# Inverting the softmax sums of a fused attention kernel: a whole-tile reciprocal, or two block transposes around a reciprocal of one column in 32

## The chip, the cores and the metric

The kernel runs on one core of a Trainium2 chip. The metric is the device time of one execution in microseconds. The engines are named as in the profile: PE (TensorE, matrix products), DVE (VectorE), ACT (ScalarE), POOL (GpSimd) and SP (SyncE, which here issues DMAs). [...]

## What is computed

Eight images of 256 channels and 32x32 points pass through two layers. Layer 0 is an attention of 8 heads of 32 channels: all 1024 points ask, and 1426 keys and values answer, which come from pooled and convolved maps. Layer 1 is an attention with one head over the 1024 points of each image, followed by eight experts of three matrix products each. The change touches only the softmax of layer 0:

```python
attn = jax.nn.softmax(jnp.einsum('bhqd,bhkd->bhqk', q_g, k) * SCALE, axis=-1)
out_att = jnp.einsum('bhqk,bhkd->bhqd', attn, v)
```

The kernel forms the exponentials without subtracting a maximum, multiplies them with the values, and divides the product by the sum of the exponentials afterwards. A checksum of the sums and of their inverses is kept (`hi` and `lo`), from which the end of the program decides whether a slower, general path has to be taken.

## The kernel before

**Units and steps.** Attention of layer 0 works through 32 units: 8 images (`b`), 2 halves of the channels (`c`, four heads each), and 2 halves of the queries (`sl`, 512 each). A unit has 11 steps, one for each block of 128 keys, and each image has one more step for the keys left over. In a step, PE forms the scores of four heads (`scores`, tile `sc`, four PSUM banks and only one such tile), ACT takes the exponential of all 2048 columns into a tile `pt`, and PE multiplies the exponentials of the step before with the values (`values`, into `pv`). The next step's scores need `sc` free, so they wait for this step's exponential.

**The sums.** The tiles `pt` are added up pairwise by DMAs that add as they write (`add`), then by DVE (`sums`, line 1571). When all are added, `sums` lets PE multiply the total with a matrix of ones, `kit.ones[:, :DH]`, one head into each group of 32 PSUM rows. So each group of 32 rows holds 32 equal copies of one head's sums for the 512 queries. This tile, `total`, takes one of the small PSUM banks: there are two with the tag `sm` and one with the tag `sx`, and every other small product uses the same three.

Before the change, ACT copies `total` to the SBUF tile `rec` and adds up the checksum on the way (line 1587). `normalise` (line 1590) inverts all 512 columns of `rec` on DVE, multiplies the unit's result `att` with it, and lets ACT run over `rec` once more for the second checksum. Then `unit` (line 1875) counts the unit as done, and after an image's last unit starts `project(b)`, the output projection, on which layer 1 of this image waits.

**The planner.** Nothing of this order is found at run time. While the program is being built, a class `Flow` keeps a clock for every engine and the state of every tile; `cost` (line 723) estimates each operation, `note` (line 765) moves the clocks and fixes each engine's order. Work beside the steps lives in generators ("threads") with a rank: the units' sums have rank 0, projection 1, keys and values 2 to 4, layer 1's output 5 and 6, the convolution's taps on DVE 7. A thread says what it needs next by a `yield`: `pe(tile)`, `ve(tile)` or `act(tile)` name the engine and the tiles that must be ready. `runnable` (line 855) lets a thread continue if the engine's planned clock is not too far ahead of PE's: at most 4.0 us for DVE and 2.0 us for ACT (`AHEAD`, line 36). For PE it asks for credit: each step gives 4.0 us to the threads of rank below 5 and 2.0 us to the others (`PACE`, `PACE1`), and lets work through without credit when the planned end of the exponential leaves PE more than 1 us to spare. A small bank counts as taken for good from its allocation until the first instruction that reads it has been planned (`open`, lines 711 and 808).

Two lines of `cost` price the operations at hand: `reciprocal` costs 0.1 + 0.0064 us for each column, and any other operation of DVE without a line of its own, a transpose too, costs 0.15 + 0.00107 us for each column.

After the steps comes the experts' stage, which begins by running the first two expert layers while layer 1 of the last image is still being worked on.

All recorded instructions have line 670 in the profile, that of the helper that calls the engine. So groups are told apart by the names of their tiles: `rec<-sm` and `rec<-sx` are ACT's copies of the sums (and, with 256 columns on DVE, layer 1's own reciprocal), `rec<-rec` is the reciprocal on DVE and the second checksum on ACT, `att<-att,rec` the product.

Of the kernel before, what the change touches and what calls it, by code (L numbers as in the profile page):

```python
# [10 lines left out]
AF = mybir.ActivationFunctionType  # L11
# [5 lines left out]
P = 128  # L17
# [3 lines left out]
DH = 32  # L21
# [891 lines left out]
def attention(tc, kit, f, outer, ended, nb, consts, x, t1, t2, hn, bounds, vecs, q_t, kv_t, proj_t, gqk_t, wqk, wqkv, vecs1, w1_d, w1c, gate_d, wrc, vecs2, bnvec):  # L913
# [6 lines left out]
    with ExitStack() as ctx:  # L920
        l1, shared = outer
        wp = ctx.enter_context(tc.tile_pool(name="w0", bufs=1))
        work = ctx.enter_context(tc.tile_pool(name="work0", bufs=1))
        psum = ctx.enter_context(tc.tile_pool(name="psum0", bufs=1, space=PSUM))

        def T(pool, shape, tag, bufs=1):
            return f.tile(pool, shape, tag, bufs=bufs)

        def small():
            if f.also and f.free("sx") < min(map(f.end, f.slots.get("sm", [None]))):  # L930
                return T(psum, [P, 512], "sx")
            return T(shared, [P, 512], "sm", bufs=2)
# [46 lines left out]
        hi, lo = bounds  # L979
        for t in bounds:  # L980
            f.pool.memset(t, 0.0)
        column = [4 * (n // 4 * 2) + n % 4 for n in range(4 * nb)]
# [108 lines left out]
        def pe(*tiles, tag=None):  # L1091
            return "PE", tiles, tag

        def ve(*tiles):
            return "DVE", tiles, None

        def act(*tiles, tag=None):
            return "ACT", tiles, tag
# [7 lines left out]
        def until(cond):  # L1106
            return None, cond, None
# [463 lines left out]
        def sums(n, pairs):  # L1571

            for i in range(1, NKC // 2):
                yield until(lambda: len(pairs) > i)
                for j in range(0, 4, 2):
                    s = pairs[0][:, j : j + 2, :]
                    yield ve(s, pairs[i])
                    f.ve.tensor_tensor(s, s, pairs[i][:, j : j + 2, :], ALU.add)
            yield until(lambda: normalised[0] == n)
            yield pe(pairs[0], tag="sm")  # L1580
            total = small()
            for j in range(4):
                f.pe.matmul(
                    total[DH * j : DH * j + DH, :], lhsT=kit.ones[:, :DH], rhs=pairs[0][:, j, :], start=True, stop=True
                )
            rec = T(work, [P, 512], "rec")
            f.act.activation(rec, total, AF.Copy, accum_out=hi[:, column[n] : column[n] + 1])
            return rec

        def normalise(b, c, sl, rec, n):  # L1590
            att = atts[b, c][:, sl]
            yield ve(rec)
            f.ve.reciprocal(rec, rec)
            f.ve.tensor_tensor(att, att, rec, ALU.mult)
            yield act(rec)
            f.act.activation(rec, rec, AF.Copy, accum_out=lo[:, column[n] : column[n] + 1])

        def project(b):
            if b == nb - 1:
                last = T(work, [P, 2, HW], "pt", bufs=6)  # L1600
                f.sp.dma_start(last, x[b].rearrange("(k p) n -> p k n", p=P))
            for m in range(2):
                for half in range(2):
                    sl = slice(half * 512, half * 512 + 512)
                    xt = last[:, m, sl] if b == nb - 1 else T(work, [P, 512], "xr")
                    yield pe(atts[b, 0], atts[b, 1], xt, tag="sm")
                    ps = small()
                    for c in range(2):
                        f.pe.matmul(
                            ps, lhsT=mt[:, c, m * P : (m + 1) * P], rhs=atts[b, c][:, sl], start=c == 0, stop=c == 1  # L1610
                        )
                    if b == nb - 1:
                        yield ve(ps, xt)
                        f.ve.scalar_tensor_tensor(xt, ps, bias[:, m : m + 1], xt, ALU.add, ALU.add)
                    else:

                        yield act(ps)
                        f.act.activation(xt, ps, AF.Identity, bias=bias[:, m : m + 1])
                        yield pool(xt)
                        f.pool.dma_start(out=t1[b][:, m, sl], in_=xt, accum_op=ALU.add)  # L1620
            if b == nb - 1:
                f.sp.dma_start(t1[b], last)
            projected[0] += 1
# [249 lines left out]
        mt = T(wp, [P, 2, C], "mt")  # L1873
        bias = T(wp, [P, 2], "mtb")
        def unit(b, c, sl, n, pairs):
            rec = yield from sums(n, pairs)
            yield from normalise(b, c, sl, rec, n)
            normalised[0] += 1
            if c and sl.start:
                f.spawn(project(b), 1)  # L1880

        atts = {}
# [21 lines left out]
        for i in range(len(steps) + 1):  # L1904
            if i < len(steps):
                b, c, half, kc = steps[i]
                sl = slice(half * 512, half * 512 + 512)
# [18 lines left out]
            if i and steps[i - 1][3] < NKC - 1:  # L1926
                b1, c1, half1, kc1 = steps[i - 1]
                if kc1 == 0:
                    pv = T(psum, [P, 512], "pv")
                    pairs = []  # L1930
                    sl1 = slice(half1 * 512, half1 * 512 + 512)
                    f.spawn(unit(b1, c1, sl1, units, pairs), 0)
                    units += 1
                f.finish(lambda: kc1 // 4 in vts[b1])
                values(b1, c1, kc1, pts[i - 1], pv)
                if kc1 % 2:
                    add(kc1, pts.pop(i - 1), pts[i - 2])
                    pairs.append(pts.pop(i - 2))
                if kc1 == NKC - 2:
                    u = 2 * c1 + half1  # L1940
                    tail_values(b1, u, pv)
                    pairs.append(pts.pop(i - 1))
                    tail_add(u, pairs[-1])
                    f.finish(lambda: projected[0] >= b1)
                    f.act.activation(atts[b1, c1][:, sl1], pv, AF.Copy)
# [510 lines left out]
def tile_conv_attn_hybrid(  # L2456
# [45 lines left out]
    with ExitStack() as early:  # L2502
        l1 = early.enter_context(tc.tile_pool(name="l1", bufs=1, side="right"))
        shared = early.enter_context(tc.tile_pool(name="psum_l1", bufs=1, space=PSUM, side="right"))
        f = Flow(tc, kit)

        ended = [0]
        attention(
            tc, kit, f, (l1, shared), ended, nb,
            consts, x, t1, t2, hn, bounds, vecs0, q_t, kv_t, proj_t, gqk_t, wqk, wqkv, vecs1, w1_d, w1c, gate_d, wrc, vecs2, bnvec,  # L2510
        )
        last(f, (l1, shared), ended, early)
# [122 lines left out]
```

## Time and profile before

| What | us |
|---|---|
| median of 3 runs | 3240.89 (3236.12 to 3240.96) |
| profiled execution | 3236.82 |
| its span, first to last instruction | 3235.0 |
| PE busy | 3064.9 (95%) |
| DVE busy | 2458.7 (76%) |
| ACT busy | 1692.2 (52%) |
| POOL busy | 1198.6 (37%) |

Attention of layer 0 lies between about 162 and 1875 us of the span. In the profile's forty slices PE stands at 7 to 9 tenths there and at 8 to 9 after it, and the granted clock of PE is at full speed but for one slice near 120 us. A group's line gives the line of code, engine and operation, the tiles, their shapes and how many there were; then, after a bar, the busy time in us and the mean of one in ns; and after a second bar the engine's idle time just before them and what ended it. A line of waits gives who waited for whom, the total in us, how often, and the longest.

### The profile page before, as it was taken

To read this page: it belongs to the slowest core of one execution; us is meant where nothing else is said; L and a number is where in the kernel's file an instruction comes from. 1 tells how busy PE (TensorE), PEld (TensorE's weight loads), DVE (VectorE), ACT (ScalarE), POOL (GpSimd) and SP (SyncE) were. 2 spreads that over 40 slices of the span, in tenths; PEclk is the share of its full clock that TensorE was granted. 3 is DMA by queue.
4 is the path that set the end of the run, shared out by engine and by line. 5 is a ranking of instruction groups with operands and counts; after the bars stand their busy time and mean duration, and the time that the engine had idled before them with its cause. 6 is when DMAs were issued, how large, how long until landed. Compare 5 with 4: busy or idle time off the path is not lost.

```text
span 3235.0 us, 55827 instructions
## 1 busy us (share of the span) xinstructions
PE 3064.9 (95%) x22342; PEld 1793.5 (55%) x22342; DVE 2458.7 (76%) x4064; ACT 1692.2 (52%) x2302; POOL 1198.6 (37%) x1293
## 2 busy tenths in 40 slices
PE   8787899999999999989999999999999999999998
PEld 3422234334334334333433367777888888888887
DVE  5787787987898889988754546346888788777776
ACT  3476676576657666676665523334333333444443
POOL 2312314214232232241111210006756666777775
PEclk9799999999999999999999999999999999999999
DMA  1277656665665565764676653124444442000000
GB/s 51 72 157 169 133 115 146 142 138 122 132 152 121 128 144 120 172 144 88 152 161 128 154 205 134 55 90 163 150 143 150 150 163 72 20 30 23 20 14 21
DMA packets 117196, 375.49 MB, mean 116 GB/s; under 512 B 14512, under 2 KB 40440, under 8 KB 93696
## 3 DMA queue, kind: packets, MB, share of 16 engines
q0 software_dynamic: 28608, 179.85, 28.7%
q1 hardware_dynamic: 84960, 190.01, 17.3%
q8 instruction: 178, 2.92, 0.4%
q10 hardware_dynamic: 3360, 1.97, 0.2%
q14 instruction: 90, 0.74, 0.1%
HBM read 118.74 MB, written 87.60 MB: 64 GB/s over the span
## 4 chain that ended last, share of the span: by engine, by line
PE 71%; DVE 10%; ACT 7%; DMA 4%; issue 4%; POOL 2%; ACTq 0%; DVEq 0%; POOLq 0%; SPq 0%
PE bank L670 22%; PE sm L670 17%; PE y L670 10%; PE sc L670 8%; PE sx L670 8%; PE pv L670 6%; ACT pt L670 5%; DMA pt<-pt 3%; DVE acc L670 3%; DVE rec L670 1%; DVE pt L670 1%; DVE h L670 1%; DMA pt<-ptail 1%; DVE c L670 1%; DVE u L670 1%
## 5 line engine op out<-in xcount | busy, mean ns | idle before, releaser
L670 ACT ACTIVATE pt<-sc 128x2048 f32<-128x2048 f32 x352 | 660.7, 1877 | 269.3 <-PE sc L670 226.8
L670 DVE SCALAR_TENSOR_TENSOR acc<-p,vec,acc 128x961 f32<-128x961 f32 (+3 forms) x960 | 554.9, 586 | 32.0 <-ACT acc L670 6.4
L670 PE MATMUL sc<-q,kn 32*128 32x512 f32 (+1 forms) x3072 | 417.3, 644 | 102.0 <-ACT pt L670 97.9
L670 DVE TENSOR_TENSOR pt<-pt,pt 128x1024 f32<-128x1024 f32 x320 | 388.1, 1260 | 125.6 <-DMA pt<-pt 110.4
L670 PE MATMUL pv<-pt,vt 128*32 128x512 f32 x2816 | 380.1, 612 | 0.1
L670 ACT ACTIVATE p1c<-bank 128x256 f32<-128x256 f32 x226 | 86.6, 383 | 556.2 <-PE bank L670 550.2
L670 ACT ACTIVATE h<-h,bnvec 128x512 f32<-128x512 f32 x452 | 341.9, 805 | 62.7 <-DVE h L670 52.6
L670 POOL DMA_DIRECT2D pt<-pt x160 | 146.1, 913 | 561.2 <-ACT pt L670 438.5
L670 POOL TENSOR_TENSOR rstd<-rstd,mhalf 128x4 f32<-128x4 f32 (+2 forms) x88 | 107.5, 1222 | 624.1 <-DVE rstd L670 592.4
L670 DVE TENSOR_TENSOR h<-p1c,bank 128x512 f32<-128x512 f32 x226 | 154.1, 682 | 222.9 <-PE bank L670 216.0
L670 PEld LDWEIGHTS sc<-q,kn 32*128 32x128 f32 (+1 forms) x3072 | 113.6, 178 | 293.4 <-ACT pt L670 195.8
L670 POOL TENSOR_TENSOR tm<-h,tm 128x256 f32<-128x256 f32 x202 | 234.7, 1162 | 15.8
L670 DVE TENSOR_TENSOR h<-u,bank 128x256 f32<-128x256 f32 x452 | 230.2, 550 | 7.8
L670 PEld LDWEIGHTS pv<-pt,vt 128*32 128x32 f32 x2816 | 55.6, 108 | 271.8 <-issue 257.1
L670 PE MATMUL bank<-h,w2e 128*128 128x256 f32 (+1 forms) x620 | 203.6, 457 | 2.8 <-DVE h L670 1.9
L670 POOL TENSOR_TENSOR tm<-h 128x512 f32<-128x512 f32 x101 | 131.8, 1304 | 189.6 <-ACT h L670 189.6
L670 DVE TENSOR_TENSOR h<-h,gate 128x1024 f32<-128x1024 f32 x128 | 199.6, 1560 | 0.5 <-ACT h L670 0.5
L670 PE MATMUL y<-t,s3e 128*128 128x256 f32 x768 | 187.0, 379 | 1.9 <-POOL t L670 1.7
L670 PE MATMUL bank<-t,s1e 128*128 128x256 f32 x750 | 182.5, 379 | 0.2 <-DVE h L670 0.2
L670 POOL TENSOR_TENSOR t<-h 128x512 f32<-128x512 f32 x104 | 135.0, 1298 | 110.3 <-DVE h L670 93.3
L670 PE MATMUL sm<-y,t 128*32 128x256 f32 (+1 forms) x1976 | 175.6, 379 | 0.1
L670 DVE TENSOR_TENSOR u<-h,bank 128x512 f32<-128x512 f32 x226 | 155.5, 688 | 24.7 <-DVE h L670 0.9
(315 smaller groups left out, 5551.8 us busy)
## 6 DMA issues: line engine op xcount, KB each, us to landing
pt<-pt POOLq DMA_DIRECT2D x160, 1024.0 KB, 7.8
h<-h SPq DMA_DIRECT2D x142, 512.0 KB
xi<-in_x_dram SPq DMA_DIRECT2D x16, 512.0 KB
t<-t SPq DMA_DIRECT2D x8, 1024.0 KB
res<-t SPq DMA_DIRECT2D x32, 256.0 KB
t<-res SPq DMA_DIRECT2D x32, 256.0 KB
hn<-res SPq DMA_DIRECT2D x32, 256.0 KB
hn<-hn SPq DMA_DIRECT2D x16, 512.0 KB
```

The costliest lines, as they stand in the source:

```text
L670: ins = fn(*args, **kwargs)
```

## The change

`sums` hands back the PSUM tile `total` and no longer copies it. `normalise` lets DVE transpose `total` into `rec`: DVE's transpose works on blocks of 32x32, so block j of a row group now has in its rows the 32 queries of that block and in each of its 32 columns the same sum. ACT then copies `total` onto itself in PSUM, which only serves the first checksum. DVE inverts one column of each block, 16 columns in all, into a small tile `one`, and transposes `one`, read 32 times over, back into all of `rec`. The product with `att` and the second checksum are unchanged.

```diff
@@ sums @@
-            rec = T(work, [P, 512], "rec")
-            f.act.activation(rec, total, AF.Copy, accum_out=hi[:, column[n] : column[n] + 1])
-            return rec
+            return total
@@ normalise @@
-        def normalise(b, c, sl, rec, n):
+        def normalise(b, c, sl, total, n):
             att = atts[b, c][:, sl]
-            yield ve(rec)
-            f.ve.reciprocal(rec, rec)
+            rec = T(work, [P, 512], "rec")
+            turned = rec.rearrange("p (j i) -> p j i", i=DH)
+            yield ve(total)
+            f.ve.transpose(rec, total)
+            f.act.activation(total, total, AF.Copy, accum_out=hi[:, column[n] : column[n] + 1])
+            one = T(work, [P, 16, 1], "one")
+            f.ve.reciprocal(one, turned[:, :, 0:1])
+            f.ve.transpose(turned, one.to_broadcast([P, 16, DH]))
             f.ve.tensor_tensor(att, att, rec, ALU.mult)
             yield act(rec)
             f.act.activation(rec, rec, AF.Copy, accum_out=lo[:, column[n] : column[n] + 1])
@@ unit @@
-            rec = yield from sums(n, pairs)
-            yield from normalise(b, c, sl, rec, n)
+            total = yield from sums(n, pairs)
+            yield from normalise(b, c, sl, total, n)
```

More of the change, by code (lines that the diff above doesn't have):

```diff
@@ L1585, in sums @@
                 )
+            return total
+        def normalise(b, c, sl, total, n):
+            att = atts[b, c][:, sl]
             rec = T(work, [P, 512], "rec")
-            f.act.activation(rec, total, AF.Copy, accum_out=hi[:, column[n] : column[n] + 1])
-            return rec
-        def normalise(b, c, sl, rec, n):
-            att = atts[b, c][:, sl]
-            yield ve(rec)
-            f.ve.reciprocal(rec, rec)
+            turned = rec.rearrange("p (j i) -> p j i", i=DH)
[5 more added lines that the diff above has]
+            f.ve.transpose(turned, one.to_broadcast([P, 16, DH]))
             f.ve.tensor_tensor(att, att, rec, ALU.mult)
```

## The prediction

> **What bounds the kernel now.** I read four views of the profile in this order: busy time by stage, the waits, the groups of instructions, and the timeline around single units. By stage (columns: window in us, its length, then busy time and instructions of each engine, granted clock, DMA share, GB/s):
>
> ```profile
> 162.00:310.00 148.00, 123.29 (x1056) 36.44 (x1052) 126.91 (x219) 105.52 (x114) 22.79 (x29) 0.98 0.77 168
> ...
> 1438.00:1663.00 225.00, 214.75 (x2218) 86.17 (x2210) 175.18 (x322) 148.37 (x186) 44.11 (x52) 1.00 0.61 132
> 1663.00:1875.00 212.00, 201.43 (x2173) 79.30 (x2170) 110.51 (x135) 116.84 (x117) 37.06 (x40) 0.99 0.66 139
> 1875.00:2190.00 315.00, 313.92 (x1231) 226.06 (x1230) 148.07 (x271) 112.49 (x196) 29.19 (x51) 0.99 0.34 121
> ```
>
> The reader is to see that PE (first pair) is nearly full everywhere, and that the last batch (1663 to 1875), where VectorE (third pair) has only 110.5 us to do, takes 212 us, hardly less than the batch before it with 175.2. VectorE's throughput doesn't pace attention. Between 162 and 1875 us PE pauses for 111 us in all (the pauses of the timeline, added up); after that it is full. PE work that finds no place in attention is done later at the same price, so only those 111 us are open to this change. What ends them:
>
> ```profile
> PE sc L670 <- ACT pt L670: 97.9, 99, 3.3
> ACT sm L670 <- DVE rec L670: 47.4, 21, 5.4
> DVE rec L670 <- ACT rec L670: 32.1, 16, 4.7
> ACT sx L670 <- DVE rec L670: 25.9, 8, 6.3
> ACT rec L670 <- DVE att L670: 16.5, 13, 3.2
> ```
>
> PE waits for the exponential of the step before (sc has one buffer). About half of these pauses are 1.0 us: a step in which the planner placed no other PE work is sc 1.14, then exp 1.88, some 3.1 us, and PE has only pv (1.06) to do beneath the exp. I call such a step bare. The groups that the change touches:
>
> ```profile
> L670 DVE RECIPROCAL rec<-rec 128x512 f32<-128x512 f32 x32 | 107.2, 3349 | 32.1 <-ACT rec L670 32.1
> L670 DVE RECIPROCAL rec<-sm 128x256 f32<-128x256 f32 x23 | 40.4, 1755 | 31.0 <-ACT sm L670 30.9
> L670 DVE TENSOR_TENSOR att<-att,rec 128x512 f32<-128x512 f32 x32 | 23.4, 732 | 1.1
> L670 DVE TENSOR_TENSOR sm<-sm,rec 128x512 f32<-128x512 f32 x20 | 13.9, 697 | 57.5 <-PE sm L670 57.5
> L670 ACT ACTIVATE rec<-rec 128x512 f32<-128x512 f32 x32 | 20.0, 626 | 16.7 <-DVE att L670 16.5
> L670 ACT ACTIVATE rec<-sm 128x512 f32<-128x512 f32 x21 | 12.5, 597 | 2.2 <-PE sm L670 2.2
> ```
>
> The last line matters most: today ScalarE's copy of the sums hardly waits for anything (2.2 us over 21 copies).
>
> [...] No transpose by VectorE is in the trace. [...]
>
> **The change part by part**, for each of the 32 units (8 batches, 2 channel halves, 2 query halves).
>
> 1. VectorE's arithmetic. Removed: one reciprocal of 512, 3.35 us. Added: a transpose of 512 columns out of PSUM, which I take at 0.70 (the sm<-sm,rec row; estimate), a reciprocal of 16 columns, and a transpose of 512 back, 0.70. The two reciprocal rows give (3349-1755)/256 = 6.2 ns a column above 160 ns, so 16 columns cost 0.26. Sum 1.66; saved 1.69, times 32 is 54 us of VectorE's time. [...] On the path this is worth little, by the last batch's 212 us.
>
> 2. The order. Before: PE's sums, ScalarE's copy (0.60 and 0.20 for the accumulator), then VectorE. After: VectorE first, then ScalarE's copy in place in PSUM at the same price (source and size alike). The product att is ready 2.5 us sooner: 0.80+3.35+0.70 becomes 1.66+0.70. In 16 units VectorE sat idle for ScalarE (32.1 us in all); that goes. What was late behind it: in unit 13 the closing ScalarE copy waits for att until 904.5, the exp starts at 905.1 and PE pauses 2.31; a bare step pauses 1.0 anyway, so 1.3 us are won. After attention's end PE has layer-1 products to do, so the sooner att wins nothing. Step 2 is worth -1 to -3; I take -1.5.
>
> 3. The new wait. ScalarE's copy now stands behind VectorE's transpose, which stands behind whatever VectorE has queued. Behind the copy on ScalarE are the next exp, on which PE's next sc waits, and evacuations of sm banks. Unit 0 shows it: sums end at 195.3, VectorE is at its taps until 198.3, so the copy ends about 195.3+2.96+0.70+0.80 = 199.8, while the exp now starts at 196.65: 3.1 us late.
>
> ```profile
> 195.37 0.60 ACT L670 ACTIVATE rec<-sm 128x512 f32<-128x512 f32 x1
> ...
> 196.65 1.88 ACT L670 ACTIVATE pt<-sc 128x2048 f32<-128x2048 f32 x1 [0.59 <-PE sc L670]
> 198.26 3.35 DVE L670 RECIPROCAL rec<-rec 128x512 f32<-128x512 f32 x1
> 198.58 0.31 PEld L670 LDWEIGHTS sc<-q,kn 32*128 32x128 f32 x8 [1.91 <-ACT pt L670]
> ```
>
> Read so at all 32, with today's order kept, the exp comes late in ten: 3.1 (unit 0), 0.9 (2), 1.8 (7), 0.6 (8), 1.6 (10), 2.0 (12), 4.0 (13), 1.1 (16), 0.6 (17), 1.5 (25); sum 17.2. The other 22 have a free VectorE or a late exp. In six of the ten (0, 2, 7, 8, 12, 17) the steps are bare and PE would feel all of it, 9.0 us; in the others two exps lie further apart and filler covers it. But the planner knows of the wait: it charges ScalarE's clock with it and puts more filler before the next sc. There is a likeness in the trace: in layer 1 ScalarE's copy waits for a reciprocal of 256 just so (the second and fourth of the waits above, 73 us over 29), and within attention I find two PE pauses behind 24 of these waits, 1.1 and 0.7. So I take half of 9.0: +4.5; bounds 0 and 17.
>
> 4. The sums' PSUM bank is held until that copy, some 1 to 4 us longer, with two sm and one sx left for all filler. Where it blocks a filler, a step turns bare, 1.0 us; between 0 and one for each unit. I take nothing, because the filler comes one step later; the cover is the two other banks.
>
> 5. New order everywhere. The planner sees VectorE 1.8 us cheaper a unit and ScalarE later, so every stream behind the first unit is dealt out anew. PE's products stay the same but for the count of plain second layers before the gates (27 now; 3.44 us plain against 3.0 otherwise, so two more or fewer are below 1 us). Which steps are bare is shuffled: unknown in sign, and I allow 8 us either way out of the 98.
>
> Sum: -1.5 + 4.5 = +3 on the profiled execution's 3236.8 (span 3235.0 and 1.8 around it), so 3239.8. The median shown, 3240.9, stands 4.1 above that execution; the same +3 on it is 3244.
>
> **The rivals.**
>
> A, the forecast: about even, 3244, own range 3234 to 3252. Chance 0.38.
>
> B, slower: ScalarE's wait in step 3 takes the place of the reciprocal and reaches PE. All ten delays count, 17.2 us: 3240.9+17 = 3258; with a bare step more in half of the units another 16, 3274. It decides once PE's wait for pt grows from 97.9 to over 105. For it: nothing hides an exp that comes late in a bare step, and VectorE is busy through most of attention. Against: the layer-1 likeness. Chance 0.37.
>
> C, faster: VectorE's queue was the hidden cause of bare steps. The chain of waits runs through the long reciprocal some eleven times; were each binding, 11 x 1.69 = 19 us, 3222; half of that, 3231. For it: the chain, and 54 + 32 us that VectorE gets back. Against: the last batch without taps is no faster, and PE's pauses at those places are 1 us or nothing. Chance 0.25.
>
> [...]
>
> **How the numbers follow.** About 0.2%, 6.5 us, is what this kernel's runs can tell from no change. A gives 0.22 of same, 0.10 slower, 0.06 faster; B 0.33 slower, 0.04 same; C 0.21 faster, 0.04 same. Together faster 0.27, same 0.30, slower 0.43. The range takes C's half and most of B: 3224 to 3268.
>
> **What would show it.** Step 1: two transposes of 0.7 and a reciprocal of 0.26 for each unit, VectorE's busy time near 2404 instead of 2459. Step 2: no VectorE wait for ScalarE's rec. Step 3: a new group of waits of ScalarE for VectorE on the sums, 30 to 70 us, and PE's wait for pt within 10 of 97.9. I am wrong if a transpose takes over 1.3, if PE's wait for pt moves by more than 15, or if attention ends before 1860 or after 1895 instead of near 1875.

## The result, and the profile after

| What | before | after |
|---|---|---|
| median | 3240.93 (3236.12 to 3246.19) | 3270.76 (3266.87 to 3277.91) |
| profiled execution | 3236.82 | 3269.62 |
| its span | 3235.0 | 3267.8 |
| attention ends (last exponential) | 1854.5 | 1877.9 |
| from there to the first product of the experts' output `y` | 356.6 | 356.6 |
| from that product to the end | 1023.9 | 1033.4 |

The medians are of four executions each, and times are in us. The ratio is 1.0096, with an interval of 1.0082 to 1.0109: the kernel became slower by about 31 us (the medians are 29.8 apart). The three last rows split the 32.8 us of the spans: 23.4 come within attention, nothing in the stretch behind it, 9.5 in the experts' stage.

First the page's line of busy times of the kernel after:

```profile
PE 3076.4 (94%) x22582; PEld 1796.1 (55%) x22582; DVE 2404.4 (74%) x4129; ACT 1688.6 (52%) x2303; POOL 1199.1 (37%) x1299
```

DVE gave back 54 us, as worked out, and PE has 11.5 us more of busy time for nearly the same products (the order moves single blocks of the experts from one form to another). Then the groups of instructions that take the place of the long reciprocal:

```profile
L670 DVE STREAM_TRANSPOSE rec<-one 128x512 f32<-128x512 f32 x32 | 22.8, 711 | 1.1
...
L670 DVE STREAM_TRANSPOSE rec<-sm 128x512 f32<-128x512 f32 x25 | 17.7, 707 | 27.9 <-PE sm L670 27.9
L670 ACT ACTIVATE sm<-sm 128x512 f32<-128x512 f32 x25 | 14.5, 582 | 41.4 <-DVE rec L670 37.4 <-DVE one L670 4.0
...
L670 DVE RECIPROCAL one<-rec 128x16 f32<-128x16 f32 x32 | 8.1, 253 | 1.1
```

The ACT line is the one to compare with before, where the copy of the sums had waited 2.2 us in 21 copies: now 25 of them wait 41.4 us, nearly all for DVE. The waits of the kernel after that bear on this:

```profile
PE sc L670 <- ACT pt L670: 104.5, 96, 3.9
ACT sm L670 <- DVE rec L670: 82.0, 39, 6.8
ACT sx L670 <- DVE rec L670: 41.1, 16, 7.0
ACT pt L670 <- DMA pt<-pt: 40.8, 17, 4.9
```

ACT's waits for DVE's `rec` (second and third line) were 73.3 us, all of them for layer 1's reciprocals, and are 123.1. But PE's wait for the exponential, the one that counts, rose only from 97.9 to 104.5, much less than 31. The last line, an exponential that waits until a DMA has freed its `pt` tile, was 28.3 us in 11 waits before.

By stage (columns as in the prediction; attention, the stretch behind it, the experts), first of the kernel before, cut at its own stage ends:

```profile
162.00:1854.50 1692.50, 1585.22 (x15862) 605.38 (x15854) 1368.73 (x2358) 1114.08 (x1333) 424.88 (x493) 0.99 0.64 139
1854.50:2211.10 356.60, 351.64 (x1364) 247.90 (x1365) 170.92 (x295) 127.76 (x222) 35.81 (x62) 0.99 0.37 129
2211.10:3235.00 1023.90, 1002.92 (x4617) 875.03 (x4615) 811.43 (x1139) 379.04 (x623) 691.21 (x670) 1.00 0.24 83
```

and then of the kernel after, cut at its own:

```profile
162.00:1878.00 1716.00, 1594.61 (x16090) 603.94 (x16086) 1315.09 (x2420) 1109.24 (x1333) 417.88 (x494) 0.99 0.64 137
1878.00:2234.50 356.50, 345.17 (x1341) 244.14 (x1342) 166.02 (x292) 124.73 (x216) 36.40 (x62) 0.98 0.36 125
2234.50:3267.00 1032.50, 1010.35 (x4645) 882.39 (x4643) 814.50 (x1143) 382.12 (x629) 698.17 (x676) 1.00 0.23 81
```

Attention's 23.5 us are 9.4 of PE busy time and 14 of pauses (window less busy time). The middle stretch keeps its length but does 6.5 us less of PE work; it has one new pause of 7.67 us at 1904 for a load of `hn`, the first expert layer's input. That work turns up in the experts' stage, where PE is busy 7.4 us longer. So the questions are why PE pauses more in attention, and why it is busy longer there.

The busy time is the clock's. In unit 0 the wait came as the prediction's step 3 foresaw, and then something more. The timeline of the kernel after (start, duration, engine, instruction; in brackets the wait before it):

```profile
197.02 0.71 DVE L670 STREAM_TRANSPOSE rec<-sm 128x512 f32<-128x512 f32 x1
197.77 0.58 ACT L670 ACTIVATE sm<-sm 128x512 f32<-128x512 f32 x1 [3.57 <-DVE rec L670]
...
198.35 1.87 ACT L670 ACTIVATE pt<-sc 128x2048 f32<-128x2048 f32 x1
...
200.27 2.09 PE L670 MATMUL sc<-q,kn 32*128 32x512 f32 x8 [3.89 <-ACT pt L670]
...
202.29 1.94 PE L670 MATMUL pv<-pt,vt 128*32 128x512 f32 x8
```

After PE's pause of 3.89 us the next scores take 2.09 us instead of 1.14 and the next product with the values 1.94 instead of 1.06: the trace's records of the granted clock have it at half from 198.8 to 205.6. The page's slices of 81 us are too coarse to show this. Between 162 us and the last 40 us of the program such stretches are 8 with 30.7 us in the trace of before and 15 with 68.3 us in the trace of after. They last 3.4 or 6.8 us each, and 7 of the 8 and 13 of the 15 begin within 8 us of the start of a pause of over 1.2 us. PE was at work for 29.4 of the 30.7 us and for 60.2 of the 68.3. Counting half of that as lost gives 14.7 and 30.1 us, an estimate of 15.4 more, which covers the whole 11.5 us by which PE's busy time rose. The additional pauses come on top (119.4 to 140.8 us behind 162 us without each program's last pause, 21.4 more).

### The profile page after: what moved, and what is told of

It reads as the page before. It is cut to its first block, busy times and chain, and to the rows that moved or that the text cites. A ratio compares the mean times of both kernels' runs of the same rounds, so it can differ in the third digit from the quotient of the medians.

```text
span 3267.8 us, 56393 instructions
## 1 busy us (share of the span) xinstructions
PE 3076.4 (94%) x22582; PEld 1796.1 (55%) x22582; DVE 2404.4 (74%) x4129; ACT 1688.6 (52%) x2303; POOL 1199.1 (37%) x1299
## 4 chain that ended last, share of the span: by engine, by line
PE 52%; DVE 4%; DMA 2%; ACT 2%; issue 2%; POOL 1%; DVEq 0%; SPq 0%; ACTq 0%; POOLq 0%
PE bank L670 22%; PE sm L670 11%; PE y L670 10%; PE sc L670 4%; PE pv L670 3%; PE sx L670 3%; DMA pt<-pt 2%; ACT pt L670 1%; DVE h L670 1%; DVE acc L670 1%; DVE c L670 1%; DVE u L670 1%; DVE pt L670 0%; DMA pt<-ptail 0%; POOL t L670 0%
## 5 line engine op out<-in xcount | busy, mean ns | idle before, releaser
L670 PE MATMUL sc<-q,kn 32*128 32x512 f32 (+1 forms) x3072 | 421.2, 652 | 107.4 <-ACT pt L670 104.5
L670 PE MATMUL sm<-p,v 128*32 128x256 f32 (+1 forms) x2728 | 213.8, 379 | 0.3 <-DVE mu L670 0.3
L670 PE MATMUL sm<-y,t 128*32 128x256 f32 (+1 forms) x2072 | 186.6, 379 | 0.0
L670 PEld LDWEIGHTS sm<-p,v 128*32 128x32 f32 (+1 forms) x2728 | 139.9, 120 | 79.0 <-issue 26.9
```

Source lines behind the costliest of these rows:

```text
L670: ins = fn(*args, **kwargs)
```

## The experiments

Each kernel was timed beside the kernel before, and its ratio refers to that. Two theories stood at first: that the new wait of ACT behind DVE is what costs (rival B of the prediction, here "the wait", and theory W in the expectations), and that the new order which the planner deals out is what costs (its step 5, "the order", theory R). A third was that the sums' PSUM bank is held too long (step 4, "the bank", theory H). The expectations call the kernels by the short names e1 to e13 that stand here in brackets.

To tell the wait from the order, a kernel must have the new instructions in the old order. For that `Flow` got a switch `blind`, under which an instruction is issued but moves no planner clock, and `note` was split so that `f.clock(...)` moves the clocks as an instruction would without issuing one.

**The change in the order of before (e1).** PE, POOL and SP issue the same sequence as before; the planner believes in the old copy and the long reciprocal.

```diff
 (sums)
-            f.act.activation(rec, total, AF.Copy, accum_out=hi[...])
-            return rec
+            f.clock("ACT", "activation", (rec, total), {"accum_out": check})
+            return rec, total
 (normalise)
             yield ve(rec)
-            f.ve.reciprocal(rec, rec)
+            f.clock("DVE", "reciprocal", (rec, rec), {})
+            f.blind = True
...
+            f.ve.transpose(rec, total)
+            f.act.activation(total, total, AF.Copy, accum_out=hi[...])
...
+            f.ve.reciprocal(one, turned[:, :, 0:1])
+            f.ve.transpose(turned, one.to_broadcast([P, 16, DH]))
+            f.blind = False
```

> The new instructions in the old order: the planner's clocks are moved as by the old reciprocal and the old copy, so every engine has the order of before, and only the new copy, transposes and small reciprocal stand in the places of the old ones. Theory W (ScalarE's wait behind VectorE reaches PE, and PE's long pauses then halve its clock): most of the loss is here, 3258 to 3275 us. Theory R (the new order dealt out by the planner costs the time, not the wait): 3236 to 3247 us.

Measured: 3265.61 us, 1.0084 (1.0067 to 1.0101). Its twin (e2) issues ACT's copy in `sums`, ahead of DVE's transpose, so that DVE waits for ACT again as before:

```diff
 (sums)
             f.clock("ACT", "activation", (rec, total), {"accum_out": check})
+            f.blind = True
+            f.act.activation(total, total, AF.Copy, accum_out=check)
+            f.blind = False
...
 (normalise)
             f.ve.transpose(rec, total)
-            f.act.activation(total, total, AF.Copy, accum_out=hi[...])
```

> As e1, but ScalarE's in-place copy of the sums comes first and VectorE's transpose after it, as in the order of before; ScalarE no longer waits for VectorE, and the PSUM bank is held until the transpose has read it. Theory W: 3236 to 3243 us, at least 15 below e1. Theory R: the same as e1 within 5 us, both near 3241.

Measured: 3234.35 us, 0.9988 (0.9979 to 0.9997). The waits of the first:

```profile
PE sc L670 <- ACT pt L670: 100.7, 91, 4.6
ACT sm L670 <- DVE rec L670: 80.3, 39, 4.1
ACT sx L670 <- DVE rec L670: 40.9, 17, 6.9
```

and of the second:

```profile
PE sc L670 <- ACT pt L670: 90.8, 90, 3.6
...
ACT sm L670 <- DVE rec L670: 44.4, 21, 3.8
...
ACT sx L670 <- DVE rec L670: 22.8, 8, 4.8
```

The arithmetic on DVE is in both. What differs is who waits, ACT for DVE in the first and DVE for ACT in the second, and that is worth 31 us between the medians (17 between the two profiled executions, whose attention ends at 1878.1 and 1860.8). The bank falls as a theory in this order: the second kernel holds it until DVE's transpose and is faster than before. So far the wait seemed to have won.

**The wait by itself, with the old arithmetic (e5),** in the order of before: DVE copies the sums out of PSUM, ACT's copy waits for that, and the long reciprocal stays.

```diff
...
+            f.ve.tensor_copy(rec, total)
+            f.act.activation(total, total, AF.Copy, accum_out=hi[...])
             f.ve.reciprocal(rec, rec)
```

> The wait without the cheap arithmetic, in the old order: VectorE copies the sums from PSUM first, ScalarE's in-place copy waits for that, and VectorE then inverts all 512 columns as before. Theory W: the loss of e1 or a little more, 3258 to 3285 us. If instead the transposes themselves cost the time (as instructions, or for what they do to PSUM), it is gone: below 3250.

Measured: 3261.27 us, 1.0064 (1.0047 to 1.0081), some 21 us over before by the ratio (23 by the medians), with no transpose in it (DVE's added copy of the sums is in those).

**The changed kernel with the copy first (e3),** as in the twin, but with the planner knowing all, so in an order of its own:

```diff
 (sums, as changed)
+            f.act.activation(total, total, AF.Copy, accum_out=hi[...])
             return total
```

> The changed kernel with its own plan, but ScalarE's in-place copy comes before VectorE's transpose, so that ScalarE doesn't wait for VectorE. Theory W: the loss goes, 3232 to 3248 us. Theory R: a new order again, so anywhere from 3235 to 3275, and no nearer to before than the changed kernel if the cheaper VectorE in the plan is the cause.

Measured: 3244.11 us, 1.0010 (0.9999 to 1.0021). Attention ends at 1863.7. It agrees with the wait, but here the wait and the order changed together.

**Only the order (e4, e8, e10, e11).** The instructions of before, with another price for the reciprocal of 512 columns in `cost`, 1.66 us in place of 3.38:

```diff
-            return 0.1 + 0.0064 * n
+            return 1.66 if n == 512 else 0.1 + 0.0064 * n
```

> The kernel before with one number of the planner changed: a reciprocal of 512 columns is planned at 1.66 us instead of 3.38, while the chip executes the same instructions. It shows what a new order alone can do. Theory W: within 8 us of 3241. Theory R: 3255 to 3275 us, since the planner now deals out as it does for the change.

Measured: 3296.54 us, 1.0177 (1.0160 to 1.0194). That is above both ranges expected, and it mixes a wrong price with a new order, so two small changes of the price followed. At 3.2 (e8):

```diff
-            return 0.1 + 0.0064 * n
+            return 3.2 if n == 512 else 0.1 + 0.0064 * n
```

> The kernel before with the reciprocal of 512 columns planned at 3.2 us instead of 3.38, which is as near to the measured 3.35: the same instructions in another order, planned as truly as before. It shows how far a new order moves the time when the plan isn't wrong. Theory W: within 8 us of 3240. Theory R: 10 us or more away.

Measured: 3292.61 us, 1.0165 (1.0148 to 1.0182). At 3.35, which is what one measures, against 3.38 planned (e10):

```diff
-            return 0.1 + 0.0064 * n
+            return 3.35 if n == 512 else 0.1 + 0.0064 * n
```

> The kernel before with the reciprocal planned at the measured 3.35 us instead of 3.38: the smallest change of plan, the same instructions. After e8 (a plan at 3.2 us lost 54) I expect that even this moves the time by 10 to 55 us upward, mostly behind the end of attention; if the loss of e8 comes from its wrong price, this stays within 8 us of 3239.

Measured: 3257.59 us, 1.0051 (1.0035 to 1.0068). And the changed kernel with DVE's transpose planned at 0.71, as measured, instead of 0.70 (e11):

```diff
+        if op == "transpose" and engine == "DVE":
+            return 0.71
```

> The changed kernel with VectorE's transpose planned at the measured 0.71 us instead of 0.70. If the loss of the change is its wait and only some 9 us are its order, this lies between 3255 and 3310 us, with attention again some 20 us later than before; if all of it were a chance of the order, it can fall to 3240.

Measured: 3294.17 us, 1.0166 (1.0149 to 1.0183). So 0.03 us in a planned price, with no instruction changed, cost 17 us, and 0.01 us in the changed kernel moved it from 31 to 54 us behind. An order is worth far more than the 8 us of step 5, and the wait's price could no longer be read from two kernels that each have an order of their own.

**The copy beside the second checksum (e6),** the planner knowing it:

```diff
 (normalise, as changed)
             f.ve.transpose(rec, total)
-            f.act.activation(total, total, AF.Copy, accum_out=hi[...])
...
             yield act(rec)
+            f.act.activation(total, total, AF.Copy, accum_out=hi[...])
             f.act.activation(rec, rec, AF.Copy, accum_out=lo[...])
```

> The changed kernel with its own plan, but ScalarE's copy of the sums is put next to its second checksum, which the planner lets go only when VectorE is done. ScalarE then hardly waits, while the PSUM bank is held longer still. Theory W: 3234 to 3252 us. Theory H (the loss is the PSUM bank that is held until ScalarE's copy, so that PE's other small products wait for it): not below the changed kernel, 3268 us or more.

Measured: 3263.36 us, 1.0067 (1.0050 to 1.0083). It falls between the ranges of both theories. Attention itself is quicker than before and ends at 1848.9, although the bank is held longest here; then 407.8 us instead of 356.6 pass to the first `y`. Of these 51.2 us more 33.6 are PE busy time, most of it work that before does later (the experts' stage is 17.0 us shorter), and 17.6 are pauses. Its timeline behind attention:

```profile
1887.07 8.93 PE L670 MATMUL bank<-hn,w1e 128*128 128x512 f32 x16 [11.38 <-DMA hn<-hn]
```

PE has run out of other work there and waits for layer 1. Three of the orders with another price take as long in this stretch (405.1, 415.2 and 407.7 us for e4, e8 and e11). Two orders can lose in two different places.

**The deciding pair: the order of after, without the wait.** A first attempt (e9) gave the changed kernel, in exactly its own order, the copy ahead of the transpose:

```diff
 (sums, as changed)
+            f.blind = True
+            f.act.activation(total, total, AF.Copy, accum_out=hi[...])
+            f.blind = False
             return total
 (normalise)
             f.ve.transpose(rec, total)
-            f.act.activation(total, total, AF.Copy, accum_out=hi[...])
+            f.clock("ACT", "activation", (total, total), {"accum_out": hi[...]})
```

> The changed kernel in its own order, instruction for instruction; only that ScalarE's in-place copy now comes before VectorE's transpose, so that VectorE waits for it and not the other way round. Theory W: attention gets back its 23 us and ends near 1855, and what the new order costs at the end of attention, some 9 us, stays: 3242 to 3254 us. Theory R (in its own order the wait is covered by what the planner put beside it, and the order is the loss): 3262 us or more.

Measured: 3279.90 us, 1.0117 (1.0100 to 1.0134). It speaks against the wait but doesn't settle it, since the wait was only turned round: DVE now waits for ACT, and the second checksum for DVE (39.9 us in place of 15.3). So in the next kernel (e12) neither waits: the first checksum is taken over the 16 transposed columns, which DVE copies to `sums16`, and at the place of the second checksum, when they have long been there. It thus sums one of each 32 equal copies instead of all of them.

```diff
             f.ve.transpose(rec, total)
-            f.act.activation(total, total, AF.Copy, accum_out=hi[...])
+            f.clock("ACT", "activation", (total, total), {"accum_out": hi[...]})
...
+            f.blind = True
+            f.ve.tensor_copy(sums16, turned[:, :, 0:1])
+            f.blind = False
...
             yield act(rec)
+            f.blind = True
+            f.act.activation(sums16, sums16, AF.Copy, accum_out=hi[...])
+            f.blind = False
             f.act.activation(rec, rec, AF.Copy, accum_out=lo[...])
```

> The changed kernel in its own order, with neither engine waiting for the other over the sums: VectorE copies the 16 columns out after its first transpose, and ScalarE sums the first checksum over these 16 columns, at the place of the second checksum. The checksum is thus taken over the transposed columns, the same sums. ScalarE has some 0.35 us less to do in each unit and the PSUM bank is free sooner. Theory W: attention gets back most of its 23 us, 3238 to 3256 us. Theory R (in its own order the loss is the order): 3262 us or more. In between, both have a share.

The same in the order of before (e13), with both checksums over 16 columns (`sums16` and `one`):

```diff
 (normalise, as in the first kernel)
-            f.act.activation(total, total, AF.Copy, accum_out=hi[...])
...
+            f.ve.tensor_copy(sums16, turned[:, :, 0:1])
...
-            f.ve.reciprocal(one, turned[:, :, 0:1])
+            f.ve.reciprocal(one, sums16)
...
-            f.act.activation(rec, rec, AF.Copy, accum_out=lo[...])
+            f.clock("ACT", "activation", (rec, rec), {"accum_out": lo[...]})
+            f.blind = True
+            f.act.activation(sums16, sums16, AF.Copy, accum_out=hi[...])
+            f.act.activation(one, one, AF.Copy, accum_out=lo[...])
+            f.blind = False
```

> The same in the order of before: two transposes, a copy and a reciprocal of 16 columns on VectorE, both checksums on ScalarE over 16 columns at the place of the second one, the planner's clocks moved as before. No wait of either engine over the sums and some 0.7 us less of ScalarE in each unit. Theory W: a little below e2, 3222 to 3234 us. If it is as e2 or slower, ScalarE's own work isn't what PE waits for.

Measured: 3271.06 us, 1.0098 (1.0077 to 1.0120), in the order of after; 3235.36 us, 0.9991 (0.9983 to 0.9999), in the order of before. The waits of the first:

```profile
PE sc L670 <- ACT pt L670: 102.0, 98, 3.4
...
ACT pt L670 <- DMA pt<-pt: 46.5, 17, 6.6
ACT sm L670 <- DVE rec L670: 42.7, 20, 5.1
ACT sx L670 <- DVE rec L670: 32.6, 10, 7.0
```

ACT's waits for DVE's `rec` are back to the 73 us of before (75.3), and nothing was won: attention ends at 1877.9, to the tenth as in the kernel after, and the later stretches are 357.0 and 1032.7 us against 356.6 and 1033.4. In unit 0 PE pauses 1.00 us instead of 3.89, and no half clock follows (the next scores take 1.14 us, not 2.09); yet the second image's first exponential starts at 310.2, no sooner than the 309.9 of the kernel after. The last image's attention begins 2.7 us sooner (1681.8 against 1684.5), and that is gone by its end. By stage, attention in the order of before and then in the order of after:

```profile
162.00:1853.40 1691.40, 1586.67 (x15842) 607.75 (x15834) 1320.63 (x2448) 1088.01 (x1332) 423.50 (x493) 0.99 0.64 138
```

```profile
162.00:1877.90 1715.90, 1597.03 (x16090) 604.97 (x16082) 1317.67 (x2450) 1098.14 (x1333) 420.06 (x494) 0.98 0.64 137
```

Between the two kernels of this pair lie 36 us. They differ in the order and in ACT's second checksum, which runs over all columns in the one and over 16 in the other; the twin above has it over all columns in the old order, at 3234.35, so the 36 us are the order's. The traces bear out that the orders are the intended ones: PE works through its tiles in the same sequence in this kernel and in the kernel after, and likewise in its fellow and in the kernel before. So for the changed kernel the wait falls, and the order holds. The bank falls in this order too: here it is free as soon as DVE has transposed it, without ACT's copy behind, and nothing was won.

Where that order loses can be read off PE's long pauses. The timeline of the kernel in the order of after, with neither wait, between 380 and 1920 us:

```profile
384.95 1.12 PE L670 MATMUL sx<-con,t 128*128 128x128 f32 x4 [5.78 <-DMA t<-t]
...
406.41 1.88 ACT L670 ACTIVATE pt<-sc 128x2048 f32<-128x2048 f32 x1 [3.84 <-DMA pt<-pt]
...
408.34 1.14 PE L670 MATMUL sc<-q,kn 32*128 32x512 f32 x8 [2.73 <-ACT pt L670]
...
1151.08 1.88 ACT L670 ACTIVATE pt<-sc 128x2048 f32<-128x2048 f32 x1 [4.99 <-DMA pt<-pt]
...
1153.01 1.14 PE L670 MATMUL sc<-q,kn 32*128 32x512 f32 x8 [2.58 <-ACT pt L670]
...
1179.07 1.88 ACT L670 ACTIVATE pt<-sc 128x2048 f32<-128x2048 f32 x1 [6.58 <-DMA pt<-pt]
...
1181.00 1.14 PE L670 MATMUL sc<-q,kn 32*128 32x512 f32 x8 [2.87 <-ACT pt L670]
...
1912.35 2.90 PE L670 MATMUL bank<-hn,w1e 128*128 128x512 f32 x3 [7.94 <-DMA hn<-hn]
```

The kernel after, which has the wait, has the same five pauses within 3 us of these places (5.55, 2.72, 2.48, 2.79 and 7.67 us). At 385 and 1912 PE itself waits for a DMA, of a tile `t` and of `hn`; before has no pause of over 1.8 us of this kind. In the three between, the exponential ahead has no free `pt` tile, since the DMA that adds an older tile into its neighbour hasn't landed. Before has this kind too, but exponentials that wait over 3 us so are 2 to 4 in the six kernels with the old order (3 in before, 4 in the one without either wait), and 6, 6 and 7 in the three with the new (6 in after and in this kernel). That bare steps in a row use up the `pt` tiles faster than the DMAs free them is my reading of these lines and wasn't tried.

**Layer 1's reciprocals too (e7).** Last, the twin above with the 256-column reciprocals of layer 1 replaced in the same way, in the order of before:

```diff
-                f.ve.reciprocal(rec, ps[:, :C])
+                f.clock("DVE", "reciprocal", (rec, ps[:, :C]), {})
+                f.blind = True
...
+                f.ve.transpose(rec, ps[:, :C])
...
+                f.ve.reciprocal(one, turned[:, :, 0:1])
+                f.ve.transpose(turned, one.to_broadcast([P, 8, DH]))
+                f.blind = False
```

> As e2, and layer 1's reciprocals of 256 columns are replaced in the same way (two transposes of 256 and a reciprocal of 8), still in the old order. VectorE saves some 0.7 us in each of 32, and ScalarE's waits for these reciprocals (73 us before) get shorter by as much. Theory W, by which waits of ScalarE count only where PE has nothing else: 3226 to 3236 us. If VectorE's queue mattered as such: below 3226.

Measured: 3234.79 us, 0.9985 (0.9978 to 0.9992). ACT's waits for DVE's `rec` fall from the 67.2 us of the twin to 52.2, and nothing comes of it: this kernel, the twin (0.9988) and the one without either wait in the old order (0.9991) lie 3 to 5 us under before and can't be told apart.

## Why the prediction was wrong

The forecast was 3244; the measurement of 3270.8 lies 3 us above the range. By the prediction's steps:

1. *DVE's arithmetic: right.* Transposes of 707 and 711 ns against 0.70, the reciprocal of 16 columns 253 ns against 0.26, DVE's busy time 2404.4 as forecast. That it is worth little on the path is right as well: in the order of before, without the new wait, it brings 3 to 5 us. But the window that was to show it reached beyond attention: the last batch's 212 us ran to 1875. Up to 1855 it took 192, 33 less than the batch before, and 29.5 of those are PE work that it had less.
2. *The order of copy and product: right in kind and small.* DVE's wait of 32.1 us for ACT's `rec` is gone, and what that is worth is contained in those 3 to 5 us.
3. *The new wait: foreseen in place and size; its cost depends on whether the planner knows of it.* ACT's waits grew by 50 us (forecast 30 to 70). Where the planner doesn't know of the wait, it costs 21 (e5, by the ratio) to 31 us (e1 against e2, by the medians), above the bound of 17; of the 17.4 us between the two profiled executions 14.7 are pauses and 3.8 longer busy time. Where it knows, as in the changed kernel, taking the wait away changes the ratio by 0.0002, with intervals of some 0.2% either way. The argument that the planner covers the wait, and the small term of 4.5, are in keeping with that.
4. *The held bank: right.* The twin holds it until DVE's transpose and is faster than before, and freeing it sooner in the order of after wins nothing.
5. *The new order everywhere: this is the step that failed.* "Unknown in sign, and I allow 8 us either way" should have been over 30: the same work is 36 us apart in the two orders. The working saw a shuffle of bare steps, pauses of 1 us, and so took their spread for small. The runs show what it left out: pauses of 2.5 to 8 us, in which an exponential waits for a DMA to free a `pt` tile or PE itself waits for a load, `hn` behind attention among them; and the half clock behind pauses, which by the estimate above (15.4 us) accounts for the 11.5 us of longer PE busy time. The signs named to tell right from wrong missed this too. PE's wait for `pt` moved by 6.6 us, within the 10 that were to mean no harm; but pauses of over 1.8 us went from 10 with 25.7 us to 16 with 51.8, while the shorter ones stayed near 90 us (93.7 and 89.0). And attention's end was named as 1875, a round stage boundary: the last exponential of before ended at 1854.5, so that 1877.9 looked harmless and was 23 us late.

Rival B came within its numbers (3258 to 3274), but not for its reason: its mechanism is real only in an order that ignores the wait. The prediction gave slower a chance of 0.43, most of it B's; that slower came is luck, and no success of that mechanism. Rival C's gain, 10 us and more, isn't there in any order tried.

On the clock the trace of before would have given a warning: between 162 us and the last 40 us, half clock began within 8 us of the start of all 3 of its pauses of over 3 us, and so it did for all 8 in after. Shorter pauses were followed so in part: of those of 1.8 to 3 us, 4 of 7 in before and 4 of 8 in after; the one of 2.31 us that ended at 907.0 in the trace of before was, the one of 2.72 us that ended at 407.8 in that of after was not.

What stays open is why this order is unlucky. Seven kernels had an order of their own (the changed one, the four with another planned price, and the two with the copy moved under the planner's eyes), and stand 3 to 57 us behind the kernel before. None is ahead, so the order of before is the best of the eight seen, and a new one was likelier to lose than "unknown in sign" says. A rival is left here: the order of after was dealt out around the wait, and may be bad for that reason, since e3, whose order knows no wait of ACT for DVE, loses only 3 us. Against it stand e4, e8 and e10, which have no such wait either and lose 17 to 57. The runs show that the order decides, and where some of the orders lose; no rule came out that would foretell it from a price.

## What to carry to other kernels

Where a program's order is dealt out at build time from estimated costs, an edit to one operation is two edits: try it once in the frozen old order, to see what the operation is worth, and once replanned, and allow for the replanning what a harmless change of a planned price by one per cent does to the time. A sum of waits says too little: list the pauses by length and by what ended them.

## What the runs showed of the hardware

In the kernel after, DVE transposes 128x512 elements of fp32 in blocks of 32x32 in 707 ns out of PSUM and in 711 ns from a source that is one column read 32 times over, 4 ns more; a product of the same size out of PSUM takes 694 ns there. The reciprocal takes 253 ns for 16 columns and 1755 for 256 in the kernel after, and 3349 for 512 in the kernel before, so inverting one column in 32 between two transposes (1671 ns together) costs half of inverting all. And PE's granted clock fell to half within otherwise busy work, for 3.4 or 6.8 us at a time in before and after, 7 of 8 times and 13 of 15 within 8 us of the start of a pause of over 1.2 us. The other way round, between 162 us and the last 40 us of before and after together, half clock began within 8 us of the start of all 11 pauses of over 3 us, of 8 of the 15 of 1.8 to 3 us, and of 2 of the 21 of 1.2 to 1.8.
